# A residual kept in DRAM during the second attention and added to by accumulating DMAs

## The chip, the cores and the metric

The kernel runs on one core of one Trainium2 chip. The core has five engines that run their own instruction queues and wait for each other through semaphores: TensorE (PE in the profile; PEld is its weight load), VectorE (DVE), ScalarE (ACT), GpSimd (POOL), and SyncE (SP), which here only issues DMAs. Matrix products read SBUF and write PSUM; DVE and ACT read both; DMAs move data between DRAM and SBUF or inside SBUF.

The metric is the device time of one execution in microseconds. Before the change it is 1589.62 us, the median of three runs (1589.33 to 1589.82).

## The reference, cut to what matters

The program is four residual layers on x of 1024 tokens by 512 channels, in float32:

```python
x = x + attn_a(layernorm(x))    # 32 heads of 16, rotary, causal
x = x + ffn(layernorm(x))       # 512x512 linear + LoRA of 2 of 8 experts chosen by a router
x = x + attn_b(layernorm(x))    # the one that is changed
x = x + ffn(layernorm(x))       # same weights as the first ffn
```

```python
def attn_b(x):                  # 32 query heads of 128 in 8 groups, one k and v head per group
    q, k, v = x @ Wq.T, x @ Wk.T, x @ Wv.T        # 4096, 1024 and 1024 columns
    q, k = rmsnorm(q, q_norm_w), rmsnorm(k, k_norm_w)
    scores = q k^T / sqrt(128) + slope[head] * (key - query), causal
    out = softmax(scores) v                        # 1024 x 4096
    return out @ Wo.T                              # back to 1024 x 512
```

The output projection sums over all 32 heads. So each group of four heads gives a 1024 by 512 part of the sum, and the residual x can take these parts one by one.

## The kernel before, in words

The tokens are cut into eight row tiles of 128. The residual is eight SBUF tiles `x0` to `x7` of 128 by 512 floats (256 KB each), made in `Block.__init__` (L74) from the pool `const`; they stay there from the first load to the last store, and each layer adds into them.

The program is written as straight Python that traces instructions; a scheduler then orders each engine's queue. In that queue the traced order is the priority, but an instruction that is ready sooner by the scheduler's own clock can be put ahead of one that is not. Two things bind it: `tc.high_priority`, and `tc.keep_in_program_order(ins)`, which puts an instruction behind the one traced before it on its engine. Once ordered, each queue runs strictly in order: an instruction that waits holds all behind it.

*First attention and FFN.* The pool `ao` ("a_out", L1179) holds two buffers that change their tenant: tag `o` (16 KB per partition) and tag `wo` (8 KB). Tag `o` has first the transposed normalized input, then the first attention's output, and from the FFN on `xnTb`, the transposed normalized input of the second attention, which is read by every k, v and q projection of all eight groups. Tag `wo` has the first output weights, then the normalized rows `xnb` and, in the second attention, each group's output weights (`load_o`, L780).

`ffn` (L585) takes a function `after(i, tp, cols)`, called when row tile i is finished, that is, after the DVE add into x (L704) in `back` (L685). In the first FFN `after` is `normalize` (L1218): it makes the normalized rows for the second attention on DVE and the transposes on PE; the transposes of the last two row tiles are left to `missing` (L1229), between the first products of the second attention.

*Second attention* (`attention_b`, L722). At its start `load_qkv(0, pinned=True)` (L786) loads the first group's weights with SP: `wkv` in two DMAs (L769) and `wq` (L775). Then come the norm weights `qw_sb` and `kw_sb` (L791, L795) and four copies that make `relr` (L797). All these are pinned with `keep_in_program_order`.

A loop runs over the eight groups g (L1088 on). The first group's k, v and q are projected ahead of it. In the loop, for each of four heads and each of eight row tiles, `softmax` computes scores on PE into PSUM (L932), adds the bias on DVE (L934), finds the maximum on DVE (L938), exponentiates on ACT (L941), and scales by 1/sum on POOL (L944). Two steps later (`LAG = 2`) `finish` transposes the result on DVE (L959, L965) and, at a head's end, multiplies it with v on PE (L993).

Between these, generators feed PE with work in units: `project_kv` of the next group (8 units), `project_o` of the group before (32 units), and `project_q` of the next group (32 units). A table `SHARE` says how many units are due after each row tile (`due`, `done`). All three write PSUM tiles of one tag, `m`, with two banks; a bank is free again when its tile was read.

`project_o(g, wo, heads, ps_m, tag, spare)` (L737) forms for each row tile t the product over the group's heads in PSUM (L742), and adds it to the residual: `nc.vector.tensor_add(self.x[t], self.x[t], ps)` on DVE (L748). Only in the second half of the last group (`spare` given) does ACT copy the PSUM tile to SBUF (L750) and POOL add it (L751).

SP issues almost all DMAs. For each half of v, `copies` (L801) makes 16 small SBUF copies (L808). The second FFN's weights are loaded in the last group (`owed`, `load_ffn`), `w_base` into the buffer of `wq`. POOL issues only the first output weights and the first FFN's weights.

*Second FFN.* Its `before` takes the last heads' `project_o`; its `after` stores the finished row tile to the output with SP.

Of the kernel before, what the change touches and what calls it, by code (L numbers as in the profile page):

```python
# [9 lines left out]
F32 = mybir.dt.float32  # L10
BF16 = mybir.dt.bfloat16
AF = mybir.ActivationFunctionType
ALU = mybir.AluOpType
# [3 lines left out]
P = 128  # L17
T = 1024
NT = T // P
C = 512  # L20
# [15 lines left out]
HKV = 8  # L36
# [26 lines left out]


class Block:
    def __init__(self, ctx, tc, x_in):
        self.tc, self.nc = tc, tc.nc
        nc = self.nc
        cp = self.cp = ctx.enter_context(tc.tile_pool(name="const", bufs=1))
        self.sm = ctx.enter_context(tc.tile_pool(name="small", bufs=4))  # L70

        self.rank = cp.tile([P, NT // 2, E], F32, tag="rank", name="rank")

        self.x = [cp.tile([P, C], F32, tag=f"x{i}", name=f"x{i}") for i in range(NT)]  # L74
        self.load_x = lambda i: nc.sync.dma_start(self.x[i], x_in[0, i * P : (i + 1) * P, :])
        for i in range(2):
            self.load_x(i)

        self.ident = cp.tile([P, P], F32, tag="ident", name="ident")
        make_identity(nc, self.ident)  # L80
        self.rel = cp.tile([P, T], F32, tag="rel", name="rel")
        self.mhalf = cp.tile([P, NT * GRP], F32, tag="mhalf", name="mhalf")
        nc.gpsimd.memset(self.mhalf, -0.5)
        nc.gpsimd.iota(
            self.rank, pattern=[[0, NT // 2], [-1, E]], base=E, channel_multiplier=0, allow_small_or_imprecise_dtypes=True
        )

    def bias(self):


        nc, rel = self.nc, self.rel
        nc.gpsimd.iota(rel, pattern=[[1, T]], base=-(T - P), channel_multiplier=-1, allow_small_or_imprecise_dtypes=True)
        nc.gpsimd.affine_select(
            out=rel, in_=rel, compare_op=ALU.is_ge, fill=NEG, base=T - P, pattern=[[-1, T]], channel_multiplier=1
        )
# [623 lines left out]
                back(i)  # L719


    def attention_b(self, ctx, wo_pool, WqT, WkT, WvT, WoT, qw, kw, xnT, missing, ffn_weights):  # L722

# [1 line left out]
        nc, tc, sm = self.nc, self.tc, self.sm  # L727
# [3 lines left out]

        cp = ctx.enter_context(tc.tile_pool(name="b_c", bufs=1))
        work = ctx.enter_context(tc.tile_pool(name="b_x", bufs=2))
        wp = ctx.enter_context(tc.tile_pool(name="b_w", bufs=1))
        oTs = {}

        def project_o(g, wo, heads, ps_m, tag, spare=None):  # L737

            for t in range(NT):
                ps = ps_m.tile([P, C], F32, tag=tag, name=f"wo{g}_{heads[0]}_{t}")  # L740
                for h in heads:
                    nc.tensor.matmul(  # L742
                        ps, lhsT=oTs[g, h][:, t * P : (t + 1) * P], rhs=wo[:, h, :], start=(h == heads[0]), stop=(h == heads[-1])
                    )
                    if h < heads[-1]:
                        yield
                if spare is None:
                    nc.vector.tensor_add(self.x[t], self.x[t], ps)  # L748
                else:
                    nc.scalar.copy(spare[:, t % 2], ps)  # L750
                    add = nc.gpsimd.tensor_tensor(self.x[t], self.x[t], spare[:, t % 2], ALU.add)  # L751
                    if t >= NT - 2:

                        tc.keep_in_program_order(add)
                yield

        with ExitStack() as ctx:
# [7 lines left out]
            def load_qkv(g, pinned=False):  # L765
                wkv = wp.tile([P, self.FFN_SMALL], F32, tag="wkv", name=f"wkv{g}")
                wkv = wkv[:, : KC * 2 * DB].rearrange("p (k n d) -> p k n d", k=KC, n=2)
                for n, src in enumerate((WkT, WvT)):
                    dma = nc.sync.dma_start(  # L769
                        wkv[:, :, n, :], src[:, g * DB : (g + 1) * DB].rearrange("(k p) n -> p k n", p=P)  # L770
                    )
                    if pinned:
                        tc.keep_in_program_order(dma)
                wq = wp.tile([P, KC, GRP * DB], F32, tag="wq", name=f"wq{g}")
                dma = nc.sync.dma_start(wq, WqT[:, g * GRP * DB : (g + 1) * GRP * DB].rearrange("(k p) n -> p k n", p=P))  # L775
                if pinned:
                    tc.keep_in_program_order(dma)
                return wq, wkv
# [265 lines left out]
            def in_turn(*gens):  # L1044
                for g in gens:
                    yield from g
# [8 lines left out]
            rest = []  # L1055
# [31 lines left out]
            for g in range(HKV):  # L1087


                last = g == HKV - 1  # L1090
                parts = [fill] if last else []
                if not last:
                    wq, wkv = load_qkv(g + 1)
                    parts.append(project_kv(g + 1, wkv))
                    parts.append(project_q(g + 1, wq))
                if last:
                    parts.append(project_o(g - 1, wo, heads, ps_m, "m"))
                elif g:
                    parts.insert(-1, project_o(g - 1, wo, heads, ps_m, "m"))
                fill = in_turn(*parts)  # L1100

                units = 72 if g else 40
                done = share = 0
                for hh in range(GRP):
                    if g and hh == 2:
                        if last:
                            for _ in fill:
                                pass
                        wo = load_o(g)
                        if last:  # L1110
                            spare = work.tile([P, T], F32, tag="w", name="spare", bufs=1).rearrange("p (a n) -> p a n", a=2)
                            fill = project_o(g, wo, heads[:2], ps_m, "m", spare)
                    for at, i in enumerate(range(NT) if last and hh == GRP - 1 else down):
                        p = softmax(g, hh, i)
                        n = hh * NT + at + 1
                        if not last:
                            share += SHARE[i]
                            due = min(units * share // (GRP * sum(SHARE)), units - (g == HKV - 2))
                        elif hh < 2:
                            due = 1 + max(0, (n - 2) * 32 // 14)  # L1120
                        else:

                            due = 33 + max(0, 14 * (n - 19) // 13)
                        while done < due:
                            next(fill, None)
                            done += 1
                            if done == 2:
                                while owed:
                                    owed.pop(0)()
                        pending.append((g, hh, i, p))  # L1130
                        if len(pending) > LAG:
                            finish(*pending.pop(0))
                    if last and hh == GRP - 1:
                        for item in pending:
                            next(fill, None)
                            finish(*item)
                if g < HKV - 2:
                    for _ in fill:
                        pass
                elif not last:  # L1140

                    owed.append(lambda: self.load_ffn(wp, nc.sync, ("wkv", "wq"), *ffn_weights))
# [12 lines left out]
def hybrid_block_kernel(  # L1155
# [18 lines left out]
    out: bass.AP,  # L1174
):
    nc = tc.nc
    blk = Block(ctx, tc, x)

    ao = ctx.enter_context(tc.tile_pool(name="a_out", bufs=1))  # L1179
    wo = ao.tile([P, KC, C], F32, tag="wo", name="a_wo")  # L1180

    def out_projection(oT, i, ps_m, tag):
# [13 lines left out]
    weights = [w_baseT, w_rhT, lora_B, b_base]  # L1196
# [8 lines left out]
    o = blk.attention_a(ao, a_wqT, a_wkT, a_wvT, rot, midway, tail)  # L1205
# [10 lines left out]
    xnT, xn = [], []  # L1216

    def normalize(i, tp, cols):  # L1218
        if not xnT:
            xnT.append(ao.tile([P, KC, T], F32, tag="o", name="xnTb"))  # L1220
            xn.append(ao.tile([P, KC, C], F32, tag="wo", name="xnb"))
        blk.normalized(i, xn[0][:, i % KC, :], "b")
        if i > 1:
            channels(i - 2, tp)
# [4 lines left out]
    def missing(n, pool, tag):  # L1229
        if 0 < n < 3:  # L1230
            channels(NT - 3 + n, pool, tag, in_order=True)

    blk.ffn("f1", projected, normalize, lag=1, parts=[slice(0, C)])
    f_ctx.close()
    rest = blk.attention_b(ctx, ao, b_WqT, b_WkT, b_WvT, b_WoT, b_qw, b_kw, xnT[0], missing, weights)
    blk.ffn(
        "f2",
        lambda work, tp, ps_m: rest(ps_m),
# [1 line left out]
        lag=2,  # L1240
        first=2,
        aside=(1, NT - 1),
        parts=[slice(0, C // 2), slice(C // 2, C)],
# [61 lines left out]
```

## Time and profile before

| what | value |
|---|---|
| device time, median of 3 runs | 1589.62 us (1589.33 to 1589.82) |
| profiled execution, span from first to last instruction | 1587.1 us (its own device time is not listed apart from the three runs) |
| PE busy | 1576.2 us, 99% |
| PEld busy | 934.3 us, 59% |
| DVE busy | 1084.9 us, 68% |
| ACT busy | 569.7 us, 36% |
| POOL busy | 364.4 us, 23% |
| DMA | 56.42 MB, 36 GB/s on average |
| granted TensorE clock, mean | 1.000 |

The stages lie in time like this: first attention 0 to 371 us, its output projection and the first FFN to 448 us, second attention to about 1522 us, second FFN to the end.

How to read the lines: an engine line gives busy us, its share of the span and the number of instructions. A line of the answer on waits gives who waited, for whom, and then the total us, how many times, and the longest. A row by stretch gives from:to, the length, then busy us (and instructions) of PE, PEld, DVE, ACT and POOL, then the granted TensorE clock as a part of full speed, the mean busy share of the 16 DMA engines, and GB/s. A line of the timeline gives the start, the duration in us, the engine, the line of the program, the operation, what it writes and reads, and how many were merged; in brackets the idle time before it and what ended it. A duration of a merged PE line runs to the modelled end of its last product, so the next line can start before it. SPq is the DMA issue on SP, not the transfer.

### The profile page before, as it was taken

The page shows a single profiled execution, that of the slowest core. Times are in us where ns is not written, and L with a number is a line of the kernel's source. Part 1 is how long each engine was busy: PE and PEld are TensorE (multiplying, and loading weights), DVE is VectorE, ACT ScalarE, POOL GpSimd, SP SyncE. Part 2 cuts the span into 40 slices and gives each one's busy share as a digit, 9 for nine tenths or more (in the row PEclk, how much of TensorE's full clock was granted, in tenths as well). Part 3 has the DMA queues.
Part 4 walks back from the last instruction along what each step waited for, and adds up shares of the span by engine and source line. Part 5 has one row for each costly group of instructions (what it writes and reads, how often), then busy time and mean ns, then how long its engine had stood idle before and what let it go on. Part 6 is the DMA issues. An engine that isn't in the chain of part 4 may idle for free.

```text
span 1587.1 us, 31573 instructions
## 1 busy us (share of the span) xinstructions
PE 1576.2 (99%) x12574; PEld 934.3 (59%) x12574; DVE 1084.9 (68%) x2841; ACT 569.7 (36%) x1397; POOL 364.4 (23%) x480
## 2 busy tenths in 40 slices
PE   9999999999999999999999999999999999999999
PEld 5545555555566557657556655756665566566654
DVE  4558788773535895775786678587667757777753
ACT  2216666664223443233233223323423322322330
POOL 3000000002222333222223213222322222222350
PEclk9999999999999999999999999999999999999999
DMA  5000332222022002002100200200110020010001
GB/s 206 1 1 6 24 20 18 20 19 63 1 72 70 20 27 68 27 1 55 40 27 28 68 27 1 73 22 28 45 49 27 27 74 28 1 54 28 2 2 53
DMA packets 66419, 56.42 MB, mean 36 GB/s; under 512 B 9504, under 2 KB 51232, under 8 KB 66272
## 3 DMA queue, kind: packets, MB, share of 16 engines
q1 hardware_dynamic: 64960, 50.46, 13.7%
q0 software_dynamic: 784, 2.90, 0.5%
q8 instruction: 99, 1.62, 0.4%
q10 hardware_dynamic: 528, 1.05, 0.2%
q14 instruction: 48, 0.39, 0.1%
HBM read 30.98 MB, written 2.10 MB: 21 GB/s over the span
## 4 chain that ended last, share of the span: by engine, by line
PE 95%; DVE 2%; POOL 1%; ACT 1%; issue 0%; DVEq 0%; ACTq 0%; POOLq 0%
PE s L932 15%; PE pq L878 14%; PE wo L742 13%; PE o L993 11%; PE sT L386 8%; PE kv L825 6%; PE oT L428 5%; PE or L993 4%; PE pm_f L693 3%; PE s L337 3%; PE pj_v L197 2%; PE pj_q L197 2%; PE pm_ao L1185 2%; PE pj_k L197 2%; PE st L910 1%; PE sT L406 1%
## 5 line engine op out<-in xcount | busy, mean ns | idle before, releaser
L941 ACT ACTIVATE p<-p,nm 128x1024 f32<-128x1024 f32 (+7 forms) x256 | 198.1, 774 | 379.9 <-DVE nm L939 362.0
L944 POOL TENSOR_SCALAR p<-p,rs 128x1024 f32<-128x1024 f32 (+7 forms) x256 | 191.0, 748 | 583.7 <-DVE rs L943 563.8
L932 PE MATMUL s<-kT,qT 128*128 128x512 f32 (+3 forms) x768 | 294.7, 492 | 0.7 <-DVE p L934 0.5
L878 PE MATMUL pq<-xnTb,wq 128*128 128x512 f32 x512 | 241.0, 596 | 0.0
L932 PEld LDWEIGHTS s<-kT,qT 128*128 128x128 f32 x768 | 141.4, 190 | 168.8 <-issue 111.4
L742 PE MATMUL wo<-wo,oT 128*128 128x512 f32 x512 | 239.7, 593 | 0.8 <-ACT spare L750 0.8
L959 DVE STREAM_TRANSPOSE pT<-p 128x512 f32<-128x512 f32 (+3 forms) x256 | 152.9, 603 | 80.3 <-PE o L993 47.4
L938 DVE TENSOR_REDUCE nm<-p 128x1 f32<-128x1024 f32 (+7 forms) x256 | 188.0, 735 | 2.8
L993 PEld LDWEIGHTS o<-pT,va 32*128 32x128 f32 x4212 | 174.4, 185 | 22.4 <-issue 11.5
L408 ACT ACTIVATE p<-sT 128x512 f32<-128x512 f32 (+1 forms) x292 | 155.2, 592 | 90.0 <-PE s L337 35.1
L993 PE MATMUL o<-pT,va 32*128 32x224 f32 (+5 forms) x4212 | 181.3, 324 | 0.0
L337 PE MATMUL s<-kT,qT 32*128 32x512 f32 (+3 forms) x768 | 164.5, 520 | 0.0
L386 PE MATMUL sT<-qT,kT 32*128 32x128 f32 (+3 forms) x1152 | 155.5, 402 | 0.4 <-ACT p L408 0.4
L742 PEld LDWEIGHTS wo<-wo,oT 128*128 128x128 f32 x512 | 94.7, 190 | 89.2 <-issue 77.2
L878 PEld LDWEIGHTS pq<-xnTb,wq 128*128 128x128 f32 x512 | 92.9, 190 | 90.0 <-issue 77.9
L934 DVE SCALAR_TENSOR_TENSOR p<-s,rq,relr 128x512 f32<-128x512 f32 x192 | 121.0, 644 | 11.3 <-PE s L932 11.2
L825 PE MATMUL kv<-wkv,xnTb 128*128 128x256 f32 x512 | 118.2, 381 | 0.2
L965 DVE STREAM_TRANSPOSE tT<-p 128x512 f32<-128x512 f32 (+3 forms) x128 | 63.9, 499 | 74.8 <-PE or L993 45.9
L934 DVE SCALAR_TENSOR_TENSOR p<-s,rq,rel 128x512 f32<-128x512 f32 (+1 forms) x192 | 103.5, 560 | 11.9 <-PE s L932 10.9
L386 PEld LDWEIGHTS sT<-qT,kT 32*128 32x128 f32 x1152 | 80.7, 184 | 50.7 <-issue 28.6
L825 PEld LDWEIGHTS kv<-wkv,xnTb 128*128 128x128 f32 x512 | 95.1, 190 | 20.9 <-issue 3.4
L354 DVE TENSOR_REDUCE part<-s 128x1 f32<-128x512 f32 x128 | 81.5, 684 | 28.2 <-PE s L337 20.1
(156 smaller groups left out, 1716.6 us busy)
## 6 DMA issues: line engine op xcount, KB each, us to landing
va<-v SPq DMA_DIRECT2D x256, 64.0 KB
wq<-in_b_WqT_dram SPq DMA_DIRECT2D x8, 1024.0 KB
wo<-in_b_WoT_dram SPq DMA_DIRECT2D x8, 1024.0 KB
x<-in_x_dram SPq DMA_DIRECT2D x8, 256.0 KB
wkv<-in_b_WkT_dram SPq DMA_DIRECT2D x8, 256.0 KB
wkv<-in_b_WvT_dram SPq DMA_DIRECT2D x8, 256.0 KB
out_dram<-x SPq DMA_DIRECT2D x7, 256.0 KB
o<-oTs SPq DMA_DIRECT2D x48, 32.0 KB
```

What stands on the lines that cost most here:

```text
L337: nc.tensor.matmul(made[j][:, at:end], lhsT=qT[rows_of(j), c, i * P : (i + 1) * P], rhs=kT[rows_of(j), c, kc * QC : kc * QC + end - at], s ...
L386: nc.tensor.matmul(made[j][:, at:end], lhsT=kT[rows_of(j), c, b * P : (b + 1) * P], rhs=qT[rows_of(j), c, qc * QC + x0 : qc * QC + x1], st ...
L408: nc.scalar.activation(p[:, j, :end], made[j][:, :end], AF.Exp)
L742: nc.tensor.matmul(ps, lhsT=oTs[g, h][:, t * P : (t + 1) * P], rhs=wo[:, h, :], start=(h == heads[0]), stop=(h == heads[-1]))
L825: nc.tensor.matmul(ps.rearrange("p a b -> p (a b)"), lhsT=xnT[:, kc, i * P : (i + 1) * P], rhs=wkv[:, kc].rearrange("p a b -> p (a b)"), s ...
L878: nc.tensor.matmul(ps, lhsT=wq[:, kc, hh * DB : (hh + 1) * DB], rhs=xnT[:, kc, cols], start=(kc == 0), stop=(kc == KC - 1))
L932: nc.tensor.matmul(s, lhsT=qT[:, i * P : (i + 1) * P], rhs=kT[:, lo:hi], start=True, stop=True)
L934: nc.vector.scalar_tensor_tensor(p[:, lo:hi], s, rq[:, i : i + 1], rels[i % 2][:, at + lo : at + hi], ALU.mult, ALU.add)
L938: nc.vector.tensor_reduce(nm, p[:, :w], AX.X, ALU.max, negate=True)
L941: nc.scalar.activation(p[:, :w], p[:, :w], AF.Exp, bias=nm, scale=slope, accum_out=ss)
L944: nc.gpsimd.tensor_scalar(p[:, :w], p[:, :w], rs, 1.0, ALU.mult, ALU.mult)
L993: nc.tensor.matmul(cols(o[:, a], j, j + skip), lhsT=vs[g][j // 4][rows, j % 4 * NB + b, :], rhs=moving(j, j + skip, rows, slice(b * B, (b ...
```

## The change

The eight tiles of x become one tile of 128 by 8 by 512 in the pool `ao`, under a new tag `x` (`hold`), until the first FFN has finished. The first FFN's `after` now also stores each finished row tile to a DRAM tile `xd`, with SP, ahead of the normalization. In the second attention the buffer of tag `x` is taken by `stage`, four staging tiles of 128 by 512.

For groups 0 to 5, whose `project_o` runs during groups 1 to 6, the DVE add of a row tile is replaced by two instructions: ACT copies the PSUM tile into a staging tile (row tile t uses tile t mod 4), and POOL issues a DMA that adds the staging tile to its rows of `xd`. That is 48 adds less on DVE, 48 copies more on ACT and 48 DMAs more on POOL.

At the start of the last group, x is made again as one tile in the buffer of tag `o`, which `xnTb` leaves then, and SP loads its eight row tiles from `xd`. From there on (`project_o` of groups 6 and 7, and the second FFN) all is as before.

```diff
@@ class Block, __init__
-        self.x = [cp.tile([P, C], F32, tag=f"x{i}", name=f"x{i}") for i in range(NT)]
+        self.xp = xp
+        self.hold(xp, "x")
         self.load_x = lambda i: nc.sync.dma_start(self.x[i], x_in[0, i * P : (i + 1) * P, :])
...
+    def hold(self, pool, tag):
+
+        x = pool.tile([P, NT, C], F32, tag=tag, name=f"x_{tag}")
+        self.x = [x[:, i] for i in range(NT)]
@@ attention_b
+        stage = wo_pool.tile([P, 4, C], F32, tag="x", name="stage")
...
-                if spare is None:
+                if g < HKV - 2:
+                    to = stage[:, t % 4]
+                    nc.scalar.copy(to, ps)
+                    nc.gpsimd.dma_start(xd[t * P : (t + 1) * P, :], to, accum_op=ALU.add)
+                elif spare is None:
                     nc.vector.tensor_add(self.x[t], self.x[t], ps)
...
                 last = g == HKV - 1
                 parts = [fill] if last else []
+                if last:
+
+                    self.hold(self.xp, "o")
+                    for t in range(NT):
+                        nc.sync.dma_start(self.x[t], xd[t * P : (t + 1) * P, :])
@@ hybrid_block_kernel
-    blk = Block(ctx, tc, x)
-
     ao = ctx.enter_context(tc.tile_pool(name="a_out", bufs=1))
+    sums = ctx.enter_context(tc.tile_pool(name="sums", bufs=1, space=bass.MemoryType.DRAM))
+    blk = Block(ctx, tc, x, ao)
...
-    blk.ffn("f1", projected, normalize, lag=1, parts=[slice(0, C)])
+    xd = sums.tile([T, C], F32, tag="xd", name="xd")
+
+    def after(i, tp, cols):
+        nc.sync.dma_start(xd[i * P : (i + 1) * P, :], blk.x[i])
+        normalize(i, tp, cols)
+
+    blk.ffn("f1", projected, after, lag=1, parts=[slice(0, C)])
     f_ctx.close()
-    rest = blk.attention_b(ctx, ao, b_WqT, b_WkT, b_WvT, b_WoT, b_qw, b_kw, xnT[0], missing, weights)
+    rest = blk.attention_b(ctx, ao, b_WqT, b_WkT, b_WvT, b_WoT, b_qw, b_kw, xnT[0], xd, missing, weights)
```

More of the change, by code (lines that the diff above doesn't have):

```diff
@@ L65, with __init__ @@
 class Block:
-    def __init__(self, ctx, tc, x_in):
+    def __init__(self, ctx, tc, x_in, xp):
         self.tc, self.nc = tc, tc.nc
@@ L719, in ffn, with attention_b @@
                 back(i)
-    def attention_b(self, ctx, wo_pool, WqT, WkT, WvT, WoT, qw, kw, xnT, missing, ffn_weights):
+    def attention_b(self, ctx, wo_pool, WqT, WkT, WvT, WoT, qw, kw, xnT, xd, missing, ffn_weights):
         nc, tc, sm = self.nc, self.tc, self.sm
```

## The prediction

> **What bounds the kernel now.** I read four views: engine shares and waits first, then a table by period, then the timeline where the change cuts in, then the ends of the run for the clock. The page's first part, and TensorE's (PE's) waits in the answer on waits (total us, times, longest):
>
> ```profile
> PE 1576.2 (99%) x12574; PEld 934.3 (59%) x12574; DVE 1084.9 (68%) x2841; ACT 569.7 (36%) x1397; POOL 364.4 (23%) x480
> PE wo L742 <- ACT spare L750: 0.8, 1, 0.8
> PE s L932 <- DVE p L934: 0.5, 2, 0.3
> ```
>
> Of the 1587.1 us span PE is idle for 1587.1 - 1576.2 = 10.9 us, and in the second attention the two waits shown, 1.3 us, are all. The busy time by stretch (length, then PE, PEld, DVE, ACT, POOL) between equal points of successive groups, and one passage of PE inside:
>
> ```profile
> 612.17:746.60 134.43, 134.40 (x960) 82.49 (x960) 96.44 (x234) 42.98 (x122) 35.28 (x46) 1.00 0.13 36
> 1149.88:1284.31 134.43, 134.40 (x961) 82.50 (x960) 96.38 (x234) 43.00 (x122) 35.29 (x46) 1.00 0.14 36
> 626.10 1.88 PE L742 MATMUL wo<-wo,oT 128*128 128x512 f32 x4
> 627.82 0.81 PE L932 MATMUL s<-kT,qT 128*128 128x384 f32 x2
> ```
>
> A period is 134.43 us with 0.03 us of PE idle. The four 512-column products start 1.72 us before the next piece, 0.43 us each: the same pace as 8 in 3.44 us in the first projections. So PE paces every group, and DVE at 96.4 of 134.4 us follows.
>
> [...]
>
> Now the seam between the first FFN and the second attention. SP's queue, then PE and DVE:
>
> ```profile
> 361.28 14.68 SPq L459 DMA_DIRECT2D o<-over  x8
> 376.06 0.53 SPq L769 DMA_DIRECT2D wkv<-in_b_WkT_dram  x1
> 376.63 0.50 SPq L769 DMA_DIRECT2D wkv<-in_b_WvT_dram  x1
> 377.18 0.51 SPq L775 DMA_DIRECT2D wq<-in_b_WqT_dram  x1
> 378.75 4.05 SPq L797 DMA_DIRECT2D relr<-rel  x4
> 454.01 0.39 SPq L782 DMA_DIRECT2D wo<-in_b_WoT_dram  x1
> 447.32 0.60 PE L109 MATMUL tp_b<-ident,xnb 128*128 128x128 f32 x4
> 447.56 0.67 DVE L704 TENSOR_TENSOR x<-x,pm_f 128x512 f32<-128x512 f32 x1
> 447.76 3.62 PE L825 MATMUL kv<-wkv,xnTb 128*128 128x256 f32 x16
> ```
>
> The first group's weights go out right behind the last DMA of the first attention, 70 us before PE uses them at 447.76. They are pinned (`pinned=True`, `keep_in_program_order`): each issues behind whatever was traced before it on SP, and today the FFN puts nothing there. DVE's add that finishes x[7] ends at 448.23, after PE is ready for those weights.
>
> **The change part by part.**
>
> *Eight stores of x to DRAM in the FFN, on SP.* SP issues nothing from 382.8 to 454.0, and the first seven are out before 447. But each waits for its row tile's last add, and the eighth is now the DMA that the pinned loads are behind. After DVE's 448.23: an output store starts 0.03 us after its add (1556.92 to 1556.95) and takes 0.33 us to issue, so the Wk load starts at 448.65, Wv 0.58 later. From such a pair's first issue to the last byte, in a later group (last two columns: DMA share, GB/s; the pair starts at 764.66):
>
> ```profile
> 764.50:765.00 0.50, 0.50 (x3) 0.36 (x2) 0.32 (x2) 0.00 (x0) 0.34 (x1) 1.00 0.56 131
> 767.50:768.00 0.50, 0.50 (x3) 0.26 (x2) 0.50 (x3) 0.34 (x2) 0.00 (x0) 1.00 0.41 119
> 768.00:768.50 0.50, 0.50 (x3) 0.22 (x2) 0.38 (x3) 0.00 (x0) 0.37 (x1) 1.00 0.00 0
> ```
>
> About 3.1 us: 451.75. With 0.25 for the semaphore and the store's bytes, kv starts at 452.0 and PE loses 452.0 - 447.76 = **4.3 us**. Low end: the first x load took 2.7 us from issue to its reader (0.73 to 3.44), so 451.35 and 3.6. High end: the 1 MB wq behind them shares the engines and they end together (wq alone: 722.93 to 727.6, 4.7 us; from its issue at 449.75), 454.45 and 6.7. Nothing else is ready for PE (every product of the first group needs kv or follows it in order), and as it has no slack later, the gap stays.
>
> *The clock after the gap.* At the end of the run PE's last product ends at 1583.5; the column ahead of the DMA share is the granted clock. The second fence is PE's start.
>
> ```profile
> 1586.00:1586.50 0.50, 0.00 (x0) 0.00 (x0) 0.00 (x0) 0.00 (x0) 0.00 (x0) 1.00 0.00 0
> 1586.50:1587.10 0.60, 0.00 (x0) 0.00 (x0) 0.00 (x0) 0.00 (x0) 0.00 (x0) 0.54 0.00 0
> ```
> ```profile
> 1.53 5.09 PE L109 MATMUL tp_i<-ident 128*128 128x128 f32 x24 [1.53 <-POOL ident masks.py:199]
> ```
>
> The clock halved 3.0 us after the last product. 24 transposes at the start took 5.09 us; at the later spacing (4 in 0.60 with a last one of 0.27, so 0.11 apart) they take 2.8: a cold start costs 2.3 us. A gap of 4.3 can trip this. Ends 0 and 2.3; I take half, **1.1**, since one drop at 3.0 can't say that every 4.3 trips.
>
> [...]
>
> *The other loads that move behind the store*: wq, qw, kw, four relr copies. wq is issued at 449.75; even queued behind 768 KB it lands by 457, and project_q starts 14.7 us after kv (462.45 - 447.76), at 466.7. relr ends its issue near 455.4 and is read after 493. SP's next, wo and the 32 va copies, wait for xnb and for v, which slip by 4.3 as well. Cost 0, cover 10 us and more.
>
> *48 DVE adds go* (L748, 0.672 us): 32.3 us of DVE, 5.4 per period. Worth 0, as PE idles 0.03 there.
>
> *48 ScalarE copies come* (0.58 us, the row of spare), 4.6 per period on ACT's 43.0. They now free PE's PSUM banks, and exponentials queue behind them. With two banks, a copy must end before PE opens the tile after next; the adds of period one are 4.2 to 11.6 us apart (627.69, 632.04, 637.43, 649.04). The eight spare copies cost PE 0.8 us once, where tiles followed 1.9 us apart. Ends 0 and 48 x 0.1 = 4.8; taken 0, by the spacing.
>
> *48 accumulating DMAs on POOL*: 256 KB issues took 0.55 to 0.60 us, the longest issue 0.98. Each waits for ACT's copy, with the scaling of p behind it, for which DVE's transposes wait. DVE already waits 58.8 us for that scaling (29.9 + 28.9) without PE idling. Ends 0 and 48 x 0.98 = 47, were all of it passed on; taken 0, since each tile also frees 0.67 us of DVE. A stage slot returns after four tiles (627.69 to 653.6, 25.9 us); POOL's loads landed in at most 10.0.
>
> *Reload in the last group, eight loads on SP*: they wait for xnT's last reader, the product before 1396.8 where w_base waits today. 8 x 0.55 = 4.4 us of issue and some 9 us of bytes end near 1408; the first add is at 1419.2. w_base slips 4.4 against a use after 1543; the va copies (1406.8) just fit. Cost 0, cover 11 us.
>
> Sum: 1587.1 + 4.3 + 1.1 = 1592.5 of span. The profiled execution's own device time isn't listed; set at the median of the runs, 1589.62, it has 2.5 us around its span: **1595.0 us**, 0.34% slower. What 3 runs tell from no change is about 0.2%, 3.2 us.
>
> **The rivals.** (A) *Hidden after all*: the weights land before 447.76. It decides if they are issued by about 444.6, ahead of the last two stores. For it: their buffers were free at 376; against: the pin. 1589.6. (B) *Stage path stalls PE as well*: a copy behind an exponential, or POOL's issue ahead of p, in groups 1 to 6. For it: the spare stall; against: 0.03 us idle and the spacing. At its price of 4.8: 1599.8. (C) *DVE's relief pays*, the other side: at the tightest spacings a period's products sum to 132.2 us (128 for q and wo at 0.43, 55.0; scores 31.0; kv 13.8; four heads of o at 5.53, 22.1; or 7.7; the small ones 2.6), 2.2 less than 134.43; were all of that DVE's, six periods give 13 and the time is 1595.0 - 13 = 1582. [...] It decides above 5.4 us.
>
> **How the numbers follow.** Forecast 0.73, A 0.11, B 0.11, C 0.05. Its own range is 3.6 to 9.0 us (6.7 + 2.3): 1593.2 to 1598.6. A has to be let in to leave out under 2 in 10, and half of B: 1589.4 to 1600.5. Slower 0.84 (forecast and B), same 0.11, faster 0.05.
>
> **What would show it.** Right: a PE idle of 4 to 7 us before the first kv, released by a DMA, with wkv's issues just behind a store of x; after it perhaps a few us of clock below 1.00 and kv products spaced double; periods still 134.4; DVE near 91 per period, ACT near 47.6; the last group unmoved. Wrong: wkv still issued near 376 (A), periods over 135 (B), or under 133.5 (C). An accumulate far slower than the loads, holding stage slots, would break the zeros.

## The result and the profile after

| what | before | after |
|---|---|---|
| device time, median (runs) | 1589.57 us (1589.33 to 1589.82, 4 runs) | 1596.23 us (1595.55 to 1597.34, 4 runs) |
| ratio to before | | 1.0042, 95% interval 1.0028 to 1.0057 |
| span of the profiled execution | 1587.1 us | 1594.1 us (its own device time 1595.91) |
| HBM written | 2.10 MB | 16.78 MB |

The change made the kernel 6.7 us slower. The page's first part of the kernel after, and the top of TensorE's waits with two further lines of that answer:

```profile
PE 1578.5 (99%) x12574; PEld 935.5 (59%) x12574; DVE 1066.1 (67%) x2793; ACT 595.0 (37%) x1445; POOL 406.0 (25%) x528
PE kv L836 <- DMA wkv<-in_b_WvT_dram: 4.6, 1, 4.6
PE wo L749 <- ACT spare L761: 0.9, 1, 0.9
PE s L943 <- DVE p L945: 0.5, 2, 0.3
```

The work moved as the code says: DVE has 48 instructions fewer and 18.8 us less, ACT 48 more and 25.3 us more, POOL 48 more and 41.6 us more. PE has the same 12574 products, but 2.3 us more of busy time, and one new wait: the first `kv` product of the second attention waits 4.6 us for its weights. The seam in the kernel after, SP's queue first, then PE:

```profile
421.76 27.30 SPq L1252 DMA_DIRECT2D xd<-x_x  x8
449.16 0.39 SPq L780 DMA_DIRECT2D wkv<-in_b_WkT_dram  x1
449.60 0.56 SPq L780 DMA_DIRECT2D wkv<-in_b_WvT_dram  x1
```
```profile
447.81 0.60 PE L115 MATMUL tp_b<-ident,xnb 128*128 128x128 f32 x4
453.00 5.38 PE L836 MATMUL kv<-wkv,xnTb 128*128 128x256 f32 x16 [4.59 <-DMA wkv<-in_b_WvT_dram]
458.22 0.60 PE L115 MATMUL tp_b<-ident,xnb 128*128 128x128 f32 x4
```

The weights are issued right behind the eighth store of x, at 449.16 instead of 376.06. Before, `kv` followed the last transposes by 0.44 us (447.32 to 447.76), and its first 16 products kept PE for 3.46 us (447.76 to 451.22). After, `kv` starts 453.00 - (447.81 + 0.44) = 4.75 us late, and the same 16 products take 458.22 - 453.00 = 5.22 us, 1.76 us longer. The granted clock, the column ahead of the DMA share, tells why (kernel after, busy time by stretch; 453.00 is where `kv` starts; the rows left out, from 454.00 to 456.00, read 0.50):

```profile
452.50:453.00 0.50, 0.00 (x0) 0.03 (x1) 0.00 (x0) 0.00 (x0) 0.00 (x0) 1.00 0.61 125
453.00:453.50 0.50, 0.50 (x2) 0.47 (x3) 0.00 (x0) 0.00 (x0) 0.00 (x0) 0.84 0.86 147
453.50:454.00 0.50, 0.50 (x2) 0.41 (x2) 0.00 (x0) 0.00 (x0) 0.00 (x0) 0.50 0.56 184
456.00:456.50 0.50, 0.50 (x3) 0.41 (x2) 0.00 (x0) 0.00 (x0) 0.00 (x0) 0.50 0.47 86
456.50:457.00 0.50, 0.50 (x3) 0.38 (x3) 0.00 (x0) 0.46 (x4) 0.00 (x0) 0.75 0.52 173
457.00:457.50 0.50, 0.50 (x4) 0.45 (x3) 0.00 (x0) 0.23 (x2) 0.00 (x0) 1.00 0.97 348
```

The rows on its two sides read 1.00 and 0.50, so a mean of 0.84 over half a microsecond is taken as half clock for the last 0.16 of it, which puts the drop at 453.34, just after the products have started; the 0.75 puts the return at 456.75, 3.41 us later. After that nothing differs in length. Two groups' periods of the kernel after:

```profile
619.15:753.57 134.42, 134.39 (x960) 82.51 (x960) 93.33 (x226) 47.21 (x130) 42.29 (x54) 1.00 0.26 52
1156.83:1291.25 134.42, 134.39 (x960) 82.52 (x960) 93.23 (x226) 47.22 (x130) 42.27 (x54) 1.00 0.26 52
```

A period is 134.42 us, as before. So the span's 7.0 us are 4.75 of gap, 1.76 of half clock, and 0.49 by which the whole run was later already ahead of the seam (its last transposes stand at 447.81 instead of 447.32). That last part doesn't look like the change's: DVE gets the first tile of x at 3.97 us instead of 3.44, and in experiments 3 to 7 below, whose code is the same up to the stores, the lateness ahead of the seam lies anywhere from -0.02 to 0.40.

### The profile page after: what moved, and what is told of

The parts are those of the page before. It is cut to its first block, busy times and chain, and to the rows that moved or that the text cites. A ratio compares the mean times of both kernels' runs of the same rounds, so it can differ in the third digit from the quotient of the medians.

```text
span 1594.1 us, 31750 instructions
## 1 busy us (share of the span) xinstructions
PE 1578.5 (99%) x12574; PEld 935.5 (59%) x12574; DVE 1066.1 (67%) x2793; ACT 595.0 (37%) x1445; POOL 406.0 (25%) x528
## 2 busy tenths in 40 slices
DMA packets 75637, 73.22 MB, mean 46 GB/s; under 512 B 10528, under 2 KB 52256, under 8 KB 75488
## 3 DMA queue, kind: packets, MB, share of 16 engines
HBM read 33.08 MB, written 16.78 MB: 31 GB/s over the span
## 4 chain that ended last, share of the span: by engine, by line
PE 94%; DVE 2%; POOL 1%; ACT 1%; issue 1%; DMA 1%; SPq 0%; DVEq 0%; ACTq 0%; POOLq 0%
PE s L943 15%; PE pq L889 14%; PE wo L749 13%; PE o L1004 11%; PE sT L392 7%; PE kv L836 6%; PE oT L434 5%; PE or L1004 4%; PE pm_f L699 3%; PE s L343 3%; PE pj_v L203 2%; PE pj_q L203 2%; PE pm_ao L1201 2%; PE pj_k L203 2%; PE st L921 1%; PE sT L412 1%
```

## The experiments

The theory: only the order on SP's queue costs anything. The pinned loads stand behind a store that waits for DVE's last add, PE stands idle until they land, and then runs at half clock for a while. The rivals: the staging path through ACT and POOL also costs PE time, or DVE's relief pays some back; and for the slow products, that they share SBUF or DMA engines with the loads that are still landing.

This table answers for all of them. From each profiled execution (the ratio from all executions, each against executions of the kernel before taken beside them): when the first `wkv` load is issued, how much later than before the last transposes ahead of `kv` start, how late `kv` is against 0.44 us after them, how much longer than 3.46 us its first 16 products take, the sum of the three, and the span less 1587.1.

| kernel | wkv issued | start | gap | products | sum | span | time, ratio to before (95%) |
|---|---|---|---|---|---|---|---|
| after | 449.16 | 0.49 | 4.75 | 1.76 | 7.00 | 7.0 | 1596.23, 1.0042 (1.0028 to 1.0057) |
| 1 stores by POOL | 376.03 | -0.01 | 0 | -0.01 | -0.02 | 0.1 | 1589.28, 1.0000 (0.9991 to 1.0010) |
| 2 stores alone | 449.32 | 0.66 | 4.79 | 2.22 | 7.67 | 7.6 | 1596.41, 1.0045 (1.0030 to 1.0059) |
| 3 two stores late | 442.92 | 0.30 | 0 | 0 | 0.30 | 0.3 | 1589.46, 1.0000 (0.9991 to 1.0009) |
| 4 one store late | 447.33 | -0.02 | 3.71 | 1.76 | 5.45 | 5.5 | 1594.09, 1.0030 (1.0017 to 1.0042) |
| 5 gap filled | 448.65 | -0.02 | 5.47 | 0.07 | 5.52 | 5.5 | 1594.23, 1.0033 (1.0020 to 1.0045) |
| 6 wq last | 449.07 | 0.40 | 4.70 | 1.76 | 6.86 | 6.9 | 1595.97, 1.0041 (1.0025 to 1.0057) |
| 7 small last store | 448.87 | 0.20 | 4.62 | 1.75 | 6.57 | 6.5 | 1596.05, 1.0042 (1.0026 to 1.0057) |
| 8 not pinned | 372.05 | 0.75 | 0 | 0 | 0.75 | 0.7 | 1589.21, 0.9999 (0.9990 to 1.0009) |

In every row the three parts give the span's difference within 0.1 us, so what the rest of the kernel has gained and lost comes to no more than that.

**1. The whole change, with the stores of x issued by POOL.**

```diff
-        nc.sync.dma_start(xd[i * P : (i + 1) * P, :], blk.x[i])
+        nc.gpsimd.dma_start(xd[i * P : (i + 1) * P, :], blk.x[i])
```

> The change with one word altered: the eight stores of x in the first FFN are issued by POOL instead of SP, so the pinned first loads of the second attention have no store ahead of them on SP. Nothing is left out. Theory 'order' (the whole loss is the loads' place behind the last store): wkv issues near 376 us again, PE's wait before the first kv goes from 4.6 us to under 0.2, the first sixteen kv products take 3.5 us instead of 5.2, and the span falls from 1594.1 to 1587.1-1587.7 (the 0.5 us by which the first load of x landed later may stay or not); time 1589.5 to 1590.3. Rival 'stage path' (ACT copies and accumulating DMAs cost as well): the stage path is whole here, so whatever it costs stays and the time is above 1591. Rival 'traffic' (the stores' bytes slow what runs beside them): the same bytes are written, so most of the loss stays, 1593 and more.

The same time as before. SP, PE and a period of this kernel:

```profile
376.03 0.53 SPq L780 DMA_DIRECT2D wkv<-in_b_WkT_dram  x1
447.75 3.62 PE L836 MATMUL kv<-wkv,xnTb 128*128 128x256 f32 x16
746.62:881.05 134.43, 134.40 (x958) 82.52 (x957) 93.24 (x226) 47.22 (x130) 42.28 (x54) 1.00 0.26 52
```

The loads go out 70 us ahead again. The copies, the 48 accumulating DMAs, the reload and DVE's relief are all still there, and together they are worth nothing that can be measured, within 0.1%. Nor do a loss and a gain cancel each other in the groups: PE is idle for 0.03 us of the period, as before. So the loss is in the place of the stores on SP.

**2. Before, with the eight stores and nothing else of the change.** Nobody reads what they store.

```diff
...
+    def after(i, tp, cols):
+        nc.sync.dma_start(xd[i * P : (i + 1) * P, :], blk.x[i])
+        normalize(i, tp, cols)
+
-    blk.ffn("f1", projected, normalize, lag=1, parts=[slice(0, C)])
+    blk.ffn("f1", projected, after, lag=1, parts=[slice(0, C)])
```

> The kernel before with one part of the change alone: the eight stores of x to DRAM by SP in the first FFN, whose rows nobody reads; x stays in eight SBUF tiles, and all adds stay on DVE. Theory 'order': a PE wait of 4.4 to 5.0 us before the first kv and some 1.8 us of half clock after it, span 1593.5 to 1594.1, time about 1596.0 - as much as the whole change. Rival 'stage path': less than the whole change, the rest belongs to the copies and accumulates. DVE stays at 96.4 us per period, the periods at 134.4.

```profile
449.32 0.39 SPq L769 DMA_DIRECT2D wkv<-in_b_WkT_dram  x1
453.21 5.84 PE L825 MATMUL kv<-wkv,xnTb 128*128 128x256 f32 x16 [4.63 <-DMA wkv<-in_b_WvT_dram]
```

The stores alone cost what the change costs. The span is 0.6 us above the expected range, through a start 0.66 later and 2.22 instead of some 1.8 us in the products. Experiments 1 and 2 settle the cause from both sides.

**3 and 4. The change, with the last two stores, or only the last, behind the pinned loads.** The number of stores moved sets when the loads go out. (`stage` is then taken a few lines later, as it has the buffer of x; not shown.) The expectation for experiment 3, two stores late, comes first.

```diff
@@ attention_b, behind the copies that make relr; NT - 1 in experiment 4
+            for i in range(NT - 2, NT):
+                tc.keep_in_program_order(nc.sync.dma_start(xd[i * P : (i + 1) * P, :], self.x[i]))
@@ after
-        nc.sync.dma_start(xd[i * P : (i + 1) * P, :], blk.x[i])
+        if i < NT - 2:
+            nc.sync.dma_start(xd[i * P : (i + 1) * P, :], blk.x[i])
```

> The change with the last two stores of x (row tiles 6 and 7) moved behind the pinned loads on SP, the other six ahead as they are. The staging tile is taken a few lines later, since it has the buffer of x. Nothing is left out. Theory 'order': the loads are now behind the store of row tile 5, whose add ends near 442.7; with the 3.8 us that the loads took from issue to PE, wkv is there at 446.9, ahead of the 448.25 at which PE comes to it: wait under 0.2 us, no slow products, span 1587.1 to 1587.7. Rival 'traffic': all eight stores still run beside the loads, a part of the loss stays (2 us and more).

> The change with only the last store of x (row tile 7) moved behind the pinned loads on SP; the staging tile is taken a few lines later. Nothing is left out. Theory 'order': the loads are now behind the store of row tile 6, whose add ends 1.3 us before that of row tile 7, so PE's wait before the first kv is 4.6 - 1.3 = 3.3 us, and the span 1587.1 + 3.5 (3.3 and about 0.2 for the start of the pipe) plus 0 to 2.3 for the clock: 1590.5 to 1593. A dose between none (two stores late, 1587.4) and the whole (1594.1). Any theory in which the place of the loads doesn't matter expects 1594.

SP and PE with two stores late, then with one:

```profile
421.60 21.23 SPq L1256 DMA_DIRECT2D xd<-x_x  x6
442.92 0.39 SPq L779 DMA_DIRECT2D wkv<-in_b_WkT_dram  x1
448.06 3.62 PE L839 MATMUL kv<-wkv,xnTb 128*128 128x256 f32 x16
```
```profile
421.27 25.97 SPq L1256 DMA_DIRECT2D xd<-x_x  x7
447.33 0.39 SPq L779 DMA_DIRECT2D wkv<-in_b_WkT_dram  x1
451.45 5.38 PE L839 MATMUL kv<-wkv,xnTb 128*128 128x256 f32 x16 [3.55 <-DMA wkv<-in_b_WvT_dram]
```

Issued at 442.92, 5.1 us ahead of `kv`, the weights are there in time. Issued behind the seventh store, at 447.33, they are 3.71 us late: about a microsecond less than behind the eighth (4.75), as the seventh row tile's add comes earlier by 1.3 us. The loss follows the time of issue.

**5. The change, with 32 transposes of the identity in the gap.** They keep PE busy, and nobody reads them.

```diff
+            for n in range(8):
+                self.transpose4(ps_s, [self.ident] * 4, f"warm{n}", tag="s", in_order=True)
             for n, _ in enumerate(in_turn(project_kv(0, wkv), project_q(0, wq))):
```

> The change with the gap on PE filled: eight times four transposes of the identity (32 products, about 0.11 us each, 3.5 us) stand ahead of the first kv in PE's queue; nobody reads them. The loads' place is unchanged, so kv still starts near 453.0. Theory 'clock' (the 1.76 us by which the first sixteen kv products were longer are a clock that the idle gap halved): no stretch of the granted clock below 1.00, the sixteen kv products take 3.5 us instead of 5.2, span 1592.3, time about 1594.4. Rival 'contention' (they were slow because wq and the rest landed in SBUF meanwhile): the loads run as before, so they stay at 5.2 us and the span at 1594.

PE, and the stretch of the first products; below it the same stretch in the kernel after:

```profile
448.58 3.71 PE L115 MATMUL tp_warm<-ident 128*128 128x128 f32 x32 [0.68 <-ACT xnTb L145]
453.21 3.69 PE L836 MATMUL kv<-wkv,xnTb 128*128 128x256 f32 x16 [0.92 <-DMA wkv<-in_b_WvT_dram]
453.00:458.30 5.30, 5.09 (x26) 4.53 (x27) 0.00 (x0) 1.87 (x9) 0.00 (x0) 1.00 0.91 221
```
```profile
453.00:458.30 5.30, 5.30 (x17) 4.33 (x18) 0.00 (x0) 0.69 (x4) 0.00 (x0) 0.68 0.76 217
```

Two idle pieces of 0.68 and 0.92 us are left, the clock stays at 1.00, and the 16 products take 3.53 us, although the DMA engines are busier (0.91 against 0.76 of their time). So it was the clock, and not the loads landing beside the products. The gap itself stays, since the weights come no sooner; here they even needed 4.56 us from issue to `kv`, which ate 0.7 us of what the clock gave back. The mended clock is worth 1.69 us in the products (1.76 less 0.07) and 2.0 by the medians, of 6.7.

**6. The change, with wq's load behind the copies of relr.** It was to tell whether wq's 1 MB slows wkv.

```diff
@@ load_qkv, ahead of wq's load
+                if pinned:
+                    return None, wkv
...
-            wq, wkv = load_qkv(0, pinned=True)
+            _, wkv = load_qkv(0, pinned=True)
@@ behind the copies that make relr
+            wq = wp.tile([P, KC, GRP * DB], F32, tag="wq", name="wq0")
+            tc.keep_in_program_order(nc.sync.dma_start(wq, WqT[:, : GRP * DB].rearrange("(k p) n -> p k n", p=P)))
```

> The change with the first group's wq load (1 MB) moved behind the relr copies in the pinned chain, so that it is issued some 4.5 us after wkv instead of 0.6 us. Nothing is left out. The loads of wkv took 3.8 us from first issue to PE in the changed kernel and 4.6 in the run with the gap filled, where 3.35 was forecast. Theory 'shared engines' (wq's bytes run between wkv's): wkv is there in 3.1 to 3.4 us, the wait falls by 0.4 to 1.2 us to about 4.0. Theory 'store ahead' (the bytes of the last store cost it): unchanged, 3.8 to 4.6 us. wq must be there by 14.7 us after kv's start, which it is by both.

wq went out at 453.60, after `kv` had begun, and wkv still took 452.86 - 449.07 = 3.79 us from its first issue to `kv` (3.84 in the kernel after). So having wq right behind isn't what makes this longer than forecast. Whether bytes that share the DMA engines do is left open: the copies of relr came in wq's place, and from the first issue to `kv` the engines moved 231 GB/s x 3.79 us = 0.88 MB here and 232 x 3.84 = 0.89 MB in the kernel after, of which wkv is 0.52. Nor does wq's delay of over 3 us cost anything.

**7. Experiment 4, with a store of 128 by 32 of the last row tile ahead of the loads.** A sixteenth of the bytes, and the same wait for DVE's add.

```diff
+        else:
+            nc.sync.dma_start(xs, blk.x[i][:, : P // 4])
```

> The change with the last store ahead of the pinned loads replaced by a small one (32 of 512 columns of row tile 7, 16 KB, into rows nobody reads); the whole store of row tile 7 follows behind the loads. Nothing is left out. The wait for the last add is the same, only the bytes ahead are fewer. Theory 'order': the loads issue at the same point, 0.9 us after the last pm_f add starts, so PE's wait stays at 4 us or more. Theory 'store ahead' for the size: wkv is there in 3.1 to 3.4 us instead of 3.8, the wait about 4.1. Theory 'shared engines': 3.8 us and 4.6 as in the change.

```profile
448.46 0.32 SPq L1259 DMA_DIRECT2D xs<-x_x  x1
448.87 0.39 SPq L779 DMA_DIRECT2D wkv<-in_b_WkT_dram  x1
452.58 5.38 PE L839 MATMUL kv<-wkv,xnTb 128*128 128x256 f32 x16 [4.45 <-DMA wkv<-in_b_WvT_dram]
```

The small store costs as much as the large one: the ratio is 1.0042 again, and the landing 3.71 us. So what costs is the wait of the store ahead of the loads, and its transfer at most the 0.13 us between 3.84 and 3.71.

**8. The change, with the first group's loads no longer pinned.**

```diff
-            wq, wkv = load_qkv(0, pinned=True)
+            wq, wkv = load_qkv(0)
```

(also `keep_in_program_order` taken off the loads of qw and kw and the copies of relr)

> The change with the pins taken off the first loads of the second attention (wkv, wq, qw, kw, relr); the scheduler then puts wkv and wq ahead of the last four copies of the first attention, and the stores behind them all. Nothing is left out. Theory 'order': no wait before the first kv, as with the stores on POOL. But 1.5 MB now go out ahead of the last o copies, for which the first attention's output projection waits: PE loses there what those copies are late, bounds 0 and 5.3 us (1.6 us of issue and 3.7 us of bytes), I expect 1 to 4. Time 1590 to 1594.

The same time as before, though all eight stores stay on SP. Its queue:

```profile
372.05 0.40 SPq L780 DMA_DIRECT2D wkv<-in_b_WkT_dram  x1
374.30 3.02 SPq L465 DMA_DIRECT2D o<-over  x4
422.04 27.28 SPq L1252 DMA_DIRECT2D xd<-x_x  x8
```

The scheduler now puts the loads among the last DMAs of the first attention. I had expected that to delay the first attention's output projection by 1 to 4 us; nothing of that size shows (a ratio of 0.9999). The 0.7 us of span lie ahead of the seam, where the output projection lies too, but 0.49 of them stand already at DVE's first tile of x (3.93 us instead of 3.44), which leaves at most some 0.3 us for it. So the stores cost nothing that can be measured by themselves: they cost because the pin ties the loads to the last of them.

Experiments 1, 3 and 8 are three ways to have the change without its loss. None is faster than before.

## Why the prediction was right, and where it was off

**PE paces the groups, so DVE's relief is worth nothing: right.** The periods stayed at 134.42 us while DVE's share fell, and experiment 1 puts the relief together with everything that replaces it at 0 within 0.1%. Rival C (1582) falls. The rows that decided it were the idle time per period (0.03 us) and the even spacing of the products (0.43 us). What the 2.2 us per period are that rival C counted on is shown by no run, but taking DVE's adds off paid none of it.

**The pinned loads fall behind the last store: right, to the microsecond.** Forecast 448.65 for the first load; with this run's later start of 0.49, 449.14; measured 449.16. From the end of DVE's last add (448.05 + 0.67 = 448.72) to the load it took 0.44 us, where 0.42 was forecast, of which the prediction's rows gave 0.36. (The seventh store is not out before 447, but at 447.24 in experiment 4; nothing hangs on it.) Rival A named the right condition as well: experiment 3, issued at 442.92, is hidden; experiment 4, at 447.33, is not. The bound of 444.6 would now be 447.76 - 3.84 = 443.9.

**The gap term, 4.3 us: mis-sized, it was 4.75.** The step that failed is "from such a pair's first issue to the last byte", 3.1 us from a later group, plus 0.25. At the seam it is 3.84 us from the first issue to `kv`; over the six kernels with a gap, 3.71 to 4.56. No row gives the 0.25. And the 3.1 stands at the low end of what the six later groups of the kernel before show for the same pair (3.05 to 3.5 us, read to the last quarter of a microsecond in which the DMA engines are a quarter busy), which may be part of the miss. Neither wq right behind (experiment 6) nor the last store's bytes (7) explain it.

Over the six kernels the time from issue to `kv` rises with what the DMA engines moved in it (0.65, 0.88, 0.89, 0.99, 1.10 and 1.16 MB in 3.71, 3.79, 3.84, 3.89, 4.12 and 4.56 us), as it would if the bytes behind wkv slowed it; but more passes in a longer time anyway, and no run leaves those bytes out, so the cause stays open.

**The clock term, 1.1 us: mis-sized, it was 1.76.** The step was "I take half, since one drop at 3.0 can't say that every 4.3 trips". Each of the five profiled gaps that were left empty tripped it (3.71, 4.62, 4.70, 4.75 and 4.79 us), and cost 1.75 to 2.22 us. The upper end, 2.3 from the start of the run, came nearer, but partly by luck: the granted clock reads 1.00 in every row of the first 8 us, so the trace doesn't show that the clock made those 24 transposes slow.

**The time around the span, 2.5 us: too much.** I set the profiled execution at the median of the runs. The profiled execution after took 1595.91 us for a span of 1594.1, so 1.8. By luck this hid part of the miss: forecast span 1592.5, measured 1594.1, of which 0.49 start, 0.45 gap, 0.66 clock. The time came out at 1596.23 for 1595.0, inside the likeliest case's own range.

**ACT's copies, POOL's DMAs and the stage slots at 0: right.** POOL waits 82.3 us in total for copies into the stage, where it costs nothing. From the answers on waits and on DMAs (issue to landing in the last column) of the kernel after:

```profile
POOL xd L757 <- ACT stage L756: 82.3, 30, 5.9
xd<-stage POOLq DMA_DIRECT2D x48, 256.0 KB, 4.1
```

A staging tile is free 4.1 us after its DMA is issued, against 25.9 us until it is needed again. Rival B (1599.8) falls with experiment 1.

**The reload in the last group at 0: right.** Its eight issues start at 1403.80 and take 3.65 us, and the first add into the new x is at 1426.14, without a wait. SP's w_base slipped to 1407.50 at no cost.

**Busy times per period:** ACT 47.2 (forecast 47.6). DVE 93.3 (forecast near 91): each add that went, 0.67 us long, freed only 3.1 / 8 = 0.39 us. The step that failed took an instruction's duration for its share of the engine. In the trace of before, an add begins 0.08 us before its forerunner ends and ends 0.08 us after its follower begins, which leaves it 0.51 to itself. The remaining 0.12 I can't place. It touched no time, as PE sets the pace, but on an engine that is the bound it would have been a gain forecast 1.7 times too large.

## What to carry to other kernels

When an edit adds a DMA to a queue, look at what is traced or pinned behind it and at what the new DMA waits for: eight stores that cost nothing themselves cost 6.5 us, because loads that had been 70 us early were tied to the last one. Relief for an engine that isn't the bound was worth nothing here, and moving its work to engines that were idle over 60% of the time cost nothing either; what decided was the order at the seam. To an idle gap of TensorE of some 4 us add the clock: 1.75 to 2.22 us in the five gaps profiled here, none in one execution by its mean clock of 1.000 (experiment 4, 1592.70 us), and up to some 3.4 by an estimate (half of the 6.83 us for which the clock was low in experiment 2).

## What the runs showed of the hardware

**The half clock began after the gap in four of the five traces with an empty gap.** In experiment 4 `kv` starts at 451.45, at full clock, and the drop comes only 1.35 us later, at 452.80 (the 0.80 in the third row; the rows left out ahead of the fourth read 0.50):

```profile
451.50:452.00 0.50, 0.50 (x3) 0.45 (x4) 0.10 (x1) 0.00 (x0) 0.00 (x0) 1.00 1.03 303
452.00:452.50 0.50, 0.50 (x4) 0.45 (x3) 0.00 (x0) 0.00 (x0) 0.00 (x0) 1.00 0.91 246
452.50:453.00 0.50, 0.50 (x4) 0.44 (x3) 0.00 (x0) 0.00 (x0) 0.00 (x0) 0.80 1.00 258
456.00:456.50 0.50, 0.50 (x4) 0.39 (x3) 0.00 (x0) 0.00 (x0) 0.00 (x0) 0.78 0.95 221
```

The drop and the return, worked out from the rows in this way for each kernel with an empty gap:

| kernel | gap | drop | after `kv` starts | return | low for |
|---|---|---|---|---|---|
| after | 4.75 | 453.34 | 0.34 | 456.75 | 3.41 |
| 2 | 4.79 | 450.74 | -2.47 | 457.57 | 6.83 |
| 4 | 3.71 | 452.80 | 1.35 | 456.22 | 3.42 |
| 6 | 4.70 | 453.47 | 0.61 | 456.88 | 3.41 |
| 7 | 4.62 | 452.81 | 0.23 | 456.22 | 3.41 |

In four of these traces the clock is low for 3.41 or 3.42 us, in experiment 2 for 6.83. There the low clock begins early, its first 2.47 us fall into the gap, and 4.36 us of it under products: hence 2.22 us lost instead of 1.76.

The waits ahead of `kv` in these five traces are 4.59, 4.63, 3.55, 4.54 and 4.45 us. In experiment 5, with idle pieces of 0.68 and 0.92 us, the clock stays at 1.00. The gap of experiment 4 doesn't seem to bring a drop in every execution: of the 21 executions of these five kernels 20 have a mean granted clock of 0.998 or 0.999, and one, of experiment 4, has 1.000; with 1592.70 us it is 1.2 us faster than the next. From what idle time on the clock drops, and what sets the moment, no run tested.

**Accumulating into DRAM was slower than storing, and cost no time here.** Experiment 1 allows the comparison, since POOL issues both there, to the same tensor and with the same 256 KB (first the answer on DMAs of experiment 1, with the landing in the last column; then a stretch of it with one plain store, and a stretch of the kernel after with one accumulating DMA):

```profile
xd<-stage POOLq DMA_DIRECT2D x48, 256.0 KB, 4.1
xd<-x_x POOLq DMA_DIRECT2D x8, 256.0 KB, 2.3
421.00:425.00 4.00, 4.00 (x11) 1.77 (x10) 3.10 (x7) 0.00 (x0) 1.62 (x3) 1.00 0.17 66
661.50:666.00 4.50, 4.50 (x12) 2.09 (x11) 3.33 (x9) 1.78 (x5) 2.28 (x3) 1.00 0.48 60
```

A DMA that adds lands in 4.1 us instead of 2.3 (medians), keeps POOL for 0.89 us instead of 0.58 (the prediction had 0.55 to 0.60, from plain issues), and its packets take 0.48 x 4.50 = 2.2 us of the 16 DMA engines instead of 0.17 x 4.00 = 0.7. Still the 16.8 MB of added traffic (73.22 MB moved, 56.42 before) cost no time.
